# A two-layer graph network on one core: sums of a set of edges kept in parts of two chunks instead of five, one PSUM bank each

## The chip, the cores and the metric

The kernel runs on one core of a Trainium2 chip. The metric is the device time of one execution in microseconds (us). TensorE (PE in the profile) multiplies matrices into PSUM, VectorE (DVE) and ScalarE (ACT) work on SBUF and PSUM, GpSimd (POOL) issues the gathers, and SyncE (SP) issues the plain loads and stores.

## The reference

There are 6250 nodes with 256 features, 106,250 directed edges sorted by their target (one of them a loop of each node), and a type from 0 to 7 on each edge. A layer norm comes first, then three layers of a relational network, then a layer norm and one layer of attention:

```python
for l in range(n_layers):                          # 3 layers, R = 8 types, D = 256
    xr = jnp.einsum('nd,rde->rne', x, W_rel[l])
    msg = xr[edge_type, src]
    agg = jax.ops.segment_sum(msg, dst, num_segments=x.shape[0])
    x = jax.nn.relu(agg + x @ W_root[l] + bias[l])
...
h = x @ Wv + bv                                    # attention over the same edges
ex = exp(leaky_relu(h[src] @ wq + h[dst] @ wk) - max over the edges of a target)
out = segment_sum(h[src] * ex / sum(ex), dst)
```

## The kernel before

The kernel sums first and multiplies by the weights afterwards: for each target node and each type it adds up the rows of the sources, and then multiplies the eight sums by the eight matrices.

**Sets and chunks.** The 106,250 edges lie in 785 chunks of at most 128. A *set* is 14 chunks (45 sets), 13 chunks (11 sets) or 12 (the last), 57 in all; its targets span at most 128 nodes. The three layers walk the same list, `order`, of (set `t`, chunk `k`). All of this stage stands in a manual schedule: every engine runs its instructions in the order in which the Python code emits them.

**One chunk** (lines 1441 to 1518). GpSimd gathers the 128 source rows (`msg`, line 1097): each row is kept as three bf16 pieces, so that the sum of the pieces has full precision. VectorE makes a matrix of ones and zeros for two chunks at a time (`make_hots`, line 1408): column 8*n + r is one for the edges with target n and type r. TensorE multiplies the rows by it (`add`, line 1432): six bf16 matmuls, two halves of the features by three pieces, that add into `bank` in PSUM. The columns that a chunk can hit are known ahead: edges are sorted and the mean number of edges per node is known, so the position of a target wanders only so far (`nodes_before`). `near[k]` is the range of nodes that chunk k of a part can hit, counted from the part's first node; it becomes wider with k, as the wander adds up. With five chunks to a part, the matmuls are 104, 152, 168, 184 and 192 columns wide.

**Parts.** A part is `PART` = 5 chunks, that add into one `bank` (two PSUM banks of 2 KB, since there are 2 x 512 columns; the pool `gps` holds two such tiles). When a part is full, VectorE adds it to the set's sums `ag` in SBUF (`evacuate`, line 1313), one chunk later. The first part starts at node 0 of the set; the others start at a node that is known only on the chip: VectorE reads it into a register (`part_of`, line 1198: a register load and two register instructions in VectorE's queue), and `ag` is addressed by that register. The 14-chunk set has three parts and two such loads. An edge of the last chunk of the set before can belong to the first node of this one: six 8-column matmuls with `hot_p` open the first part.

**The rest of a set**, spread over the chunks that follow:

- `own_rows` (lines 1295 to 1305): chunk 0 and 1: TensorE turns the set's own rows (`pt`), ScalarE copies them (`x_t`, line 1298); chunks 2 to 4: eight VectorE instructions (line 1303) write the loops' share into `ag`. The additions of the parts come after them on VectorE.
- `finish(t)` (lines 1316 to 1379), while the chunks of set t+1 run: from chunk 2 to 10, two fp32 matmuls behind each chunk (lines 1335 and 1339; each shows as two matmuls in the profile), that read `ag`; at chunk 11 VectorE adds the bias (`v`, line 1344), then ScalarE and VectorE in turn make the three bf16 pieces (lines 1347 to 1353), which SyncE stores into the table of the next layer. In the last layer the second layer norm and the attention's columns are made here.
- In layer 0, besides: `count_loops`, and `norm_split` for one or two chunks of a set whose rows come from the input directly.

**Between layers.** The first set of a layer needs rows that the last set of the layer before makes. Its edges to the last 128 nodes are left out of its gathers and are counted apart in layer 0 (`count_late`) and added in set 1 of layers 1 and 2 (`add_late`).

Of the kernel before, what the change touches and what calls it, by code (L numbers as in the profile page):

```python
# [10 lines left out]
F32 = mybir.dt.float32  # L11
BF16 = mybir.dt.bfloat16
I32 = mybir.dt.int32
AF = mybir.ActivationFunctionType
ALU = mybir.AluOpType
AX = mybir.AxisListType
PSUM = bass.MemoryType.PSUM
DRAM = bass.MemoryType.DRAM

P = 128  # L20
# [8 lines left out]
LAST = 12  # L29
MORE = 20  # L30
PART = 5
SPREAD = 4.25
# [408 lines left out]
def kernel(  # L441
# [19 lines left out]
    nc = tc.nc  # L461
    N, D = x.shape
    E = src.shape[0]
    L, R = w_rel.shape[0], w_rel.shape[1]
    KH = D // P
# [225 lines left out]
    with tc.tile_pool(name="prep", bufs=1) as prep, \  # L691
# [80 lines left out]
        for n in ranges:  # L772
# [3 lines left out]
            for k, (lo, hi) in enumerate(ranges[n]):  # L776
                nc.gpsimd.memset(lows[n][:, k:k + 1], float(R * lo))
                nc.gpsimd.memset(lows_n[n][:, k:k + 1], float(ranges_w[n][k][0]))
                nc.gpsimd.memset(wides[n][:, k:k + 1], float(R * (hi - lo)))

        zero = nw.tile([P, 3 * D], BF16, bufs=1)
        nc.gpsimd.memset(zero, 0.0)
# [108 lines left out]
        def tables():  # L891
# [18 lines left out]
            firsts = prep.tile([1, NA, NW], F32)  # L910
            nc.vector.memset(firsts[:, 1:, NW - 1:], 0.0)
            nc.vector.tensor_copy(firsts[:, 0, :], base)
            for at, view, k in by_window(dst_t):
                for a in range(1, -(-k // PART)):
                    nc.vector.tensor_scalar_mul(firsts[:, a, at], view[0:1, :, a * PART], 1.0 / R)
            part_f = prep.tile([1, NA, NW], F32)
            nc.vector.tensor_tensor(part_f, firsts, base.unsqueeze(1).to_broadcast([1, NA, NW]),
                                    ALU.subtract)
            nc.vector.tensor_copy(part_i, part_f)
            b_ps = prep_ps.tile([P, NA, NW], F32)  # L920
            nc.tensor.matmul(b_ps.rearrange("p a w -> p (a w)"), ones[0:1],
# [8 lines left out]
            for (at, l_v, n), (_, d_v, _), (_, sg_v, _), (_, st_v, _), (_, o_v, _) in zip(  # L930
                    by_window(loc), by_window(dst_t), by_window(seg), by_window(seg_t),
                    by_window(over)):
                shape = [P, at.stop - at.start, n]
                nc.vector.scalar_tensor_tensor(
                    l_v, d_v, 1.0 / R, base_b[:, at].unsqueeze(2).to_broadcast(shape),
                    op0=ALU.mult, op1=ALU.subtract)
                for k in range(0, n, PART):
                    z = min(k + PART, n)
                    nc.vector.tensor_tensor(
                        sg_v[:, :, k:z], st_v[:, :, k:z],  # L940
                        seg_b[:, k // PART, at].unsqueeze(2).to_broadcast(shape[:2] + [z - k]),
                        ALU.subtract)
                nc.vector.tensor_tensor(sg_v, sg_v, lows[n].unsqueeze(1).to_broadcast(shape),
                                        ALU.subtract)
                nc.vector.tensor_tensor(o_v, sg_v, wides[n].unsqueeze(1).to_broadcast(shape),
                                        ALU.subtract)
                yield 1.5
# [19 lines left out]
            def at_most(a: bass.AP, most: float):  # L967
                v = next(vs)
                v = viol[:a.shape[0], v:v + 1]
                nc.vector.tensor_reduce(v, a, AX.X if len(a.shape) == 2 else AX.XY, ALU.max)  # L970
                nc.vector.tensor_scalar_add(v, v, -(most + 0.5))

            def at_least(a: bass.AP, least: float):
                v = next(vs)
                v = viol[:a.shape[0], v:v + 1]
                nc.vector.tensor_reduce(v, a, AX.X if len(a.shape) == 2 else AX.XY, ALU.min)
                nc.vector.tensor_scalar(v, v, -1.0, least - 0.5, op0=ALU.mult, op1=ALU.add)
# [36 lines left out]

            for a in range(1, NA):
                at_least(part_f[:, a, :NW - 1], float(far[a][0]))
                at_most(part_f[:, a, :NW - 1], float(far[a][1]))
            row = prep.tile([1, NW], F32)
# [66 lines left out]
    def ordered_path():  # L1085
# [23 lines left out]
        with ExitStack() as s:  # L1109
# [6 lines left out]
            one = s.enter_context(tc.tile_pool(name="ones", bufs=1))  # L1116
            gps = s.enter_context(tc.tile_pool(name="gps", bufs=2, space=PSUM))
            ops = s.enter_context(tc.tile_pool(name="ops", bufs=1, space=PSUM))
# [3 lines left out]
            FROM, UPTO = 2, CW - 3  # L1122
            STEPS = UPTO + 3
            RAW = 6

# [29 lines left out]
            nc.vector.tensor_scalar_add(seg_e, seg_e, -1e6)  # L1155
            late = one.tile([P, len(parts_e), P * R // 2], BF16)

# [26 lines left out]
            def add_late(a: int, xl, ag: bass.AP):  # L1184

                m = ranges[sizes[0]][parts_e[a][-1]][1]
                at = None if a == 0 else part_of(0, a)
                for h, name in zip(range(KH), ("pl", "pt")):
                    bank = ops.tile([P, P * R // 2], F32, name=name)
                    for s_ in range(3):  # L1190
                        nc.tensor.matmul(bank[:, :R * m], xl[:, s_, h * P:(h + 1) * P],
                                         late[:, a, :R * m], start=(s_ == 0), stop=(s_ == 2))
                    to = ag[:, h, :, :m] if at is None else ag[:, h, :, ds(at, m)]
                    nc.vector.tensor_tensor(
                        to, to, bank[:, :R * m].rearrange("p (n r) -> p r n", r=R), ALU.add)

# [119 lines left out]
            def finish(l: int, at, x_t: bass.AP, x0, ag: bass.AP, t: int):  # L1316
# [5 lines left out]
                if last and x0 is None:  # L1322
                    x0 = rp.tile([P, D], F32, name="x0")
                    nc.sync.dma_start(x0, x[ds(at, P), :])
                for _ in range(FROM if t or l == 0 else FROM + len(parts_e)):
                    yield
# [101 lines left out]
            def add(bank, msg, hot, lo: int, hi: int, begin: bool):  # L1428

                for h in range(KH):  # L1430
                    for s_ in range(3):
                        nc.tensor.matmul(  # L1432
                            bank[:, h, lo:hi], msg[:, s_, h * P:(h + 1) * P],
                            hot[:, :hi - lo], start=(begin and s_ == 0), stop=False,
                            skip_group_check=True)
# [3 lines left out]
            for l in range(L):  # L1439
                ahead = None  # L1440
                for i, (t, k) in enumerate(order):
# [18 lines left out]
                    if k % PART == 0:  # L1460
                        bank = gps.tile([P, KH, P * R // 2], F32, name="bank")

# [16 lines left out]

                    for c in to_copy:  # L1480
                        evacuate(*c)
                    to_copy = []
                    if k % PART == 0:
                        part_at = None if k == 0 else part_of(t, k // PART)
                    if k % PART == PART - 1 or k == n - 1:
                        to_copy.append((bank, ag, part_at, hi))
                    if l == 0 and final and k % 3 == 1 and k // 3 < len(parts_e):
                        count_late(k // 3)
                    if l and t == 0 and k == n - 1:
                        xl = rp.tile([P, 3, D], BF16, name="xl")  # L1490
                        nc.sync.dma_start(xl.rearrange("p s d -> p (s d)"), tab[l][LATE:N, :])
                        ag_e = ag
                    if l and t == 1 and 0 <= k - FROM < len(parts_e):
                        add_late(k - FROM, xl, ag_e)
                    if l == 0:
# [158 lines left out]
```

## Time and profile before

| | |
|---|---|
| time, three runs | median 5172.17 us (5154.45 to 5180.04) |
| profiled execution | 5168.06 us; its span 5166.3 us |
| granted TensorE clock, whole span | 0.859 |
| busy over the span | PE 3790.3 us, DVE 2766.0, ACT 1061.1, POOL 3044.0 |
| additions of parts (line 1313) | 513, mean 897 ns |
| chunk matmuls (line 1432) | 13668 recorded, 1362.7 us busy |

A *busy* time is the union of an engine's instructions, without register and queue instructions. In a group, the figures behind the bar are the busy time, the mean length of one in ns, and the idle time of the engine just before, with what ended it. In a timeline, the bracket is the idle time before an instruction and what ended it ("issue": nothing that the profile shows). The three layers run from about 235 to 3745 us, the attention from there to the end; before them lies the preparation of the edges.

### The profile page before, as it was taken

To read this page: it belongs to the slowest core of one execution; us is meant where nothing else is said; L and a number is where in the kernel's file an instruction comes from. 1 tells how busy PE (TensorE), PEld (TensorE's weight loads), DVE (VectorE), ACT (ScalarE), POOL (GpSimd) and SP (SyncE) were. 2 spreads that over 40 slices of the span, in tenths; PEclk is the share of its full clock that TensorE was granted. 3 is DMA by queue.
4 is the path that set the end of the run, shared out by engine and by line. 5 is a ranking of instruction groups with operands and counts; after the bars stand their busy time and mean duration, and the time that the engine had idled before them with its cause. 6 is when DMAs were issued, how large, how long until landed. Compare 5 with 4: busy or idle time off the path is not lost. (4 is left out here: it accounts for less than half of the span.)

```text
span 5166.3 us, 80833 instructions
## 1 busy us (share of the span) xinstructions
PE 3790.3 (73%) x28813; PEld 3179.2 (62%) x28813; DVE 2766.0 (54%) x7200; ACT 1061.1 (21%) x2620; POOL 3044.0 (59%) x3293
## 2 busy tenths in 40 slices
PE   0288888888687787778688888888845666666666
PEld 0277777777566666666566666666635655565556
DVE  5577766666344444444355555555534554555555
ACT  4421111111000000000000000000024444444444
POOL 6466666665566666666566666666555555555553
PEclk5599999999789999999888888889967887888888
DMA  4555555554455555555455555555533333333332
GB/s 120 191 149 150 149 151 148 171 167 140 123 150 151 149 153 149 149 150 150 130 152 160 159 157 158 158 159 159 137 86 89 93 90 91 96 94 97 92 98 62
DMA packets 302153, 694.32 MB, mean 134 GB/s; under 512 B 62677, under 2 KB 164501, under 8 KB 301739
## 3 DMA queue, kind: packets, MB, share of 16 engines
q0 software_dynamic: 188032, 562.89, 39.8%
q1 hardware_dynamic: 112650, 125.11, 7.8%
q8 instruction: 229, 3.75, 0.3%
q14 instruction: 186, 1.52, 0.1%
q10 hardware_dynamic: 1056, 1.05, 0.1%
HBM read 634.06 MB, written 54.78 MB: 133 GB/s over the span
## 5 line engine op out<-in xcount | busy, mean ns | idle before, releaser
L1097 POOL DMA_INDIRECT msg<-tab,src_t x2252 | 2166.1, 962 | 1312.9 <-PE bank L1432 520.1
L1432 PE MATMUL bank<-hots,msg 128*128 128x104 bf16 (+4 forms) x13668 | 1362.7, 241 | 250.7 <-issue 170.6
L1432 PEld LDWEIGHTS <-msg 128*128 128x128 bf16 x14556 | 1119.4, 102 | 641.5 <-issue 388.1
L1335 PE MATMUL po<-raws,ag 128*128 128x256 f32 x3648 | 1093.5, 427 | 172.2 <-DVE hots L1408 61.9
L1097 POOL DMA_INDIRECT head<-hx,src_t x785 | 745.2, 949 | 643.2 <-ACT qm L1564 189.3
L1313 DVE TENSOR_TENSOR ag<-ag,bank 128x768 f32<-128x768 f32 x513 | 460.1, 897 | 803.1 <-PE bank L1432 579.8
L1335 PEld LDWEIGHTS po<-raws,ag 128*128 128x128 f32 x3648 | 693.2, 211 | 273.1 <-issue 75.4
L1303 DVE SCALAR_TENSOR_TENSOR ag<-loops,x_t 128x256 f32<-128x256 bf16 x1368 | 494.9, 420 | 390.6 <-issue 289.2
L1408 DVE TENSOR_TENSOR hots<-up,seg 128x304 bf16<-128x304 f32 (+4 forms) x1182 | 585.5, 506 | 32.6 <-PE bank L1432 17.6
L1335 PE MATMUL po<-wr,ag 128*128 128x256 f32 x1824 | 544.4, 422 | 38.7 <-issue 19.6
L1594 PE MATMUL pf<-ex,head 128*128 128x128 f32 x3364 | 486.5, 312 | 101.1 <-issue 55.5
L1594 PEld LDWEIGHTS pf<-ex,head 128*128 128x128 f32 x3364 | 472.0, 227 | 114.6 <-issue 60.5
L1335 PEld LDWEIGHTS po<-wr,ag 128*128 128x128 f32 x1824 | 332.9, 203 | 82.4 <-issue 31.7
L1564 ACT ACTIVATE qm<-other,head 128x128 f32<-128x128 f32 x841 | 283.1, 396 | 108.1 <-issue 42.0
L1570 DVE TENSOR_REDUCE tops<-pq 128x1 f32<-128x512 f32 x228 | 154.9, 679 | 217.4 <-ACT c L1569 161.4
L1566 PE MATMUL pq<-ident,qm 128*128 128x128 f32 x898 | 186.4, 316 | 114.7 <-issue 44.5
L563 ACT ACTIVATE std<-mv,eps 128x1 f32<-128x1 f32 x134 | 39.6, 296 | 1089.0 <-DVE mv L561 724.9
L1347 ACT ACTIVATE hml<-v 128x256 bf16<-128x256 f32 x114 | 47.6, 418 | 1023.4 <-issue 756.1
L1555 DVE TENSOR_SCALAR other<-up,loc 128x128 f32<-128x128 f32 x785 | 237.8, 341 | 13.2 <-ACT qm L1564 6.9
L1585 PE MATMUL pe<-ident,c 128*128 128x128 f32 x898 | 162.9, 325 | 94.6 <-issue 51.9
L1602 PE MATMUL po<-wv_s,fs 128*128 128x256 f32 x228 | 87.8, 523 | 190.4 <-ACT fs L1599 127.6
L1566 PEld LDWEIGHTS pq<-ident,qm 128*128 128x128 f32 x898 | 127.1, 160 | 161.0 <-ACT qm L1564 77.2
(259 smaller groups left out, 3133.3 us busy)
## 6 DMA issues: line engine op xcount, KB each, us to landing
msg<-tab,src_t POOLq DMA_INDIRECT x2252
xt<-tab SPq DMA_DIRECT2D x171, 192.0 KB
tab<-hml SPq DMA_DIRECT2D x114, 192.0 KB
head<-hx,src_t POOLq DMA_INDIRECT x785
tab<-hml SPq DMA_DIRECT2D x12, 768.0 KB
hx<-row SPq DMA_DIRECT2D x57, 128.5 KB
mine<-hx SPq DMA_DIRECT2D x57, 128.5 KB
xa<-x SPq DMA_DIRECT2D x57, 128.0 KB
```

Of the source, the lines that this page charges most:

```text
L1097: nc.gpsimd.indirect_dma_start(out=to, out_offset=None, in_=table[:upto, :], in_offset=bass.IndirectOffsetOnAxis(ap=index, axis=0))
L1303: nc.vector.scalar_tensor_tensor(ag[:, :, r, :m], loops[:, t, :m].unsqueeze(1).to_broadcast([P, KH, m]), float(r + 1), x_t[:, :, :m], op0= ...
L1313: nc.vector.tensor_tensor(to, to, bank[:, :, :R * m].rearrange("p h (n r) -> p h r n", r=R), ALU.add)
L1335: nc.tensor.matmul(po[:m], ag[:, h, r, :m], wr[:, h, r, :], start=(r == 0 and h == 0), stop=False, skip_group_check=True)
L1408: nc.vector.tensor_tensor(pair[:, :n, :width], up[:, :width].unsqueeze(1).to_broadcast([P, n, width]), of[:, i:i + n].unsqueeze(2).to_broa ...
L1432: nc.tensor.matmul(bank[:, h, lo:hi], msg[:, s_, h * P:(h + 1) * P], hot[:, :hi - lo], start=(begin and s_ == 0), stop=False, skip_group_c ...
L1555: nc.vector.tensor_scalar(other[:, :m], up[:, :m], refs[j][1], None, op0=ALU.not_equal)
L1564: nc.scalar.activation(qm[:, :m], other[:, :m], AF.Identity, scale=MASKED, bias=refs[j][0][:, D:HX])
L1566: nc.tensor.transpose(pq[:m, i, :], qm[:, :m], ident)
L1570: nc.vector.tensor_reduce(tops[:m, g:g + 1], flat, AX.X, ALU.max)
L1585: nc.tensor.transpose(pe[:, i, :m], c_t[:m, j * P:(j + 1) * P], ident[:m, :m])
L1594: nc.tensor.matmul(pf[:, h, :m], refs[j][0][:, h * P:(h + 1) * P], ex[:, i, :m], start=(j == 0 and h == 0), stop=(j == len(refs) - 1 and h ...
```

## The change

A part has two chunks. Its columns fit one PSUM bank, and four such tiles are in hand instead of two of two banks. A 14-chunk set has seven parts, so seven additions and six register loads. Parts of the current set wait until chunk 5 (`READY`), when the own rows are in place; from then on at most one part is added in a chunk. Late edges are counted two parts, and added three parts, in one chunk step, and both halves of a late part share one PSUM tile. The checks of the parts' first nodes are reduced over all parts at once.

```diff
-PART = 5
+PART = 2
...
-            gps = s.enter_context(tc.tile_pool(name="gps", bufs=2, space=PSUM))
+            gps = s.enter_context(tc.tile_pool(name="gps", bufs=4, space=PSUM))
...
+            READY = 5
...
-                for h, name in zip(range(KH), ("pl", "pt")):
-                    bank = ops.tile([P, P * R // 2], F32, name=name)
+                bank = ops.tile([P, P * R // 2], F32, name=("pl", "pt")[a % 2])
+                bank = bank.rearrange("p (h c) -> p h c", h=KH)
+                for h in range(KH):
...
+                evacuate(bank, ag, at, m)
...
-                for _ in range(FROM if t or l == 0 else FROM + len(parts_e)):
+                for _ in range(FROM if t or l == 0 else FROM + LATE_STEPS):
...
-                            hot[:, :hi - lo], start=(begin and s_ == 0), stop=False,
+                            hot[:, :hi - lo], start=(begin and h == 0 and s_ == 0), stop=False,
...
-                        bank = gps.tile([P, KH, P * R // 2], F32, name="bank")
+                        bank = gps.tile([P, KH, P * R // 4], F32, name="bank")
...
-                    for c in to_copy:
-                        evacuate(*c)
-                    to_copy = []
+                    for c in to_copy[:len(to_copy) if k < READY else 1]:
+                        if k >= READY or c[1] is not ag:
+                            evacuate(*c)
+                            to_copy.remove(c)
                     if k % PART == 0:
                         part_at = None if k == 0 else part_of(t, k // PART)
                     if k % PART == PART - 1 or k == n - 1:
                         to_copy.append((bank, ag, part_at, hi))
-                    if l == 0 and final and k % 3 == 1 and k // 3 < len(parts_e):
-                        count_late(k // 3)
+                    if l == 0 and final and k % 3 == 1:
+                        for a in range(k // 3 * 2, min(k // 3 * 2 + 2, len(parts_e))):
+                            count_late(a)
...
-                    if l and t == 1 and 0 <= k - FROM < len(parts_e):
-                        add_late(k - FROM, xl, ag_e)
+                    if l and t == 1 and 0 <= k - FROM < LATE_STEPS:
+                        for a in range((k - FROM) * 3, min((k - FROM) * 3 + 3, len(parts_e))):
+                            add_late(a, xl, ag_e)
```

`near` is computed from `PART`; its two ranges are now 0 to 13 and 3 to 22 nodes, so the chunk matmuls are 104 and 152 columns wide in turn, and a full part has 2 x 176 columns (352) where it had 2 x 384 (768).

## The prediction

> **What bounds the kernel now.** I read the page's rows of 40 slices first, then the table by stage, then the waits of one layer, then one set of that layer in order of time.
>
> ```profile
> 235.00:1285.00 1050.00, 913.55 (x7935) 766.08 (x7935) 713.61 (x1760) 167.88 (x495) 653.57 (x677) 0.94 0.54 153
> 1401.00:2502.00 1101.00, 881.87 (x6930) 715.29 (x6928) 520.97 (x1167) 76.18 (x212) 697.21 (x728) 0.93 0.53 150
> 2617.00:3730.00 1113.00, 911.18 (x6931) 749.54 (x6929) 604.51 (x1646) 80.33 (x212) 700.85 (x728) 0.88 0.58 158
> ```
>
> These are layers 0, 1 and 2 without their seams: length, busy PE, PEld, DVE, ACT, POOL, then granted clock, DMA share, GB/s. TensorE is busiest (80 to 87%), but nothing is full: gathers fill 62 to 63% of GpSimd, VectorE is at 47 to 68%. So a loop of waits sets the pace. The longest waits of TensorE in layer 1:
>
> ```profile
> PE bank L1432 <- issue: 125.4, 242, 1.3
> PE po L1335 <- DVE hots L1408: 46.1, 28, 2.0
> PE bank L1432 <- DMA msg<-tab,src_t: 3.1, 4, 1.2
> ```
>
> The columns are us in total, times, longest. One set of that layer, by start and length in us:
>
> ```profile
> 1998.10 2.07 PE L1335 MATMUL po<-raws,ag 128*128 128x256 f32 x4 [1.59 <-DVE hots L1408]
> 2002.03 0.37 ACT L1298 COPY x_t<-pt 128x256 f32<-128x256 f32 x1 [5.64 <-PE bank L1432]
> 2005.81 0.96 DVE L1313 TENSOR_TENSOR ag<-ag,bank 128x768 f32<-128x768 f32 x1
> 2007.95 0.64 PE L1432 MATMUL bank<-hots,msg 128*128 128x184 bf16 x6
> 2009.32 0.66 PE L1432 MATMUL bank<-hots,msg 128*128 128x192 bf16 x6
> 2010.71 0.44 PE L1432 MATMUL bank<-hots,msg 128*128 128x104 bf16 x6
> 2010.98 1.09 PE L1339 MATMUL po<-raws,x_t 128*128 128x256 f32 x4
> 2012.63 0.95 DVE L1313 TENSOR_TENSOR ag<-ag,bank 128x768 f32 x1 [4.12 <-PE bank L1432]
> 2013.64 0.17 PE L1432 MATMUL bank<-hot_p,msg 128*128 128x8 bf16 x1 [0.26 <-issue]
> 2015.59 0.42 DVE L1344 TENSOR_TENSOR v<-po,raws 128x256 f32<-128x256 f32 x1 [2.00 <-remote]
> 2017.44 0.43 DVE L1353 TENSOR_TENSOR hml<-v,hml 128x256 bf16<-128x256 f32 x1 [0.47 <-ACT hml L1351]
> 2018.25 0.81 DVE L1313 TENSOR_TENSOR ag<-ag,bank 128x640 f32 x1
> 2019.12 0.79 PE L1335 MATMUL po<-raws,ag 128*128 128x256 f32 x1 [1.14 <-DVE hots L1408]
> ```
>
> Gathers are no limit (3.1 us in a layer). The set shows the loop. `finish` starts at 1998.10 and its last matmuls end at 2012.07 (14.0 us); `v` on VectorE starts at 2015.59 (3.5 us later); from there VectorE makes `v` and `hml` and then adds the last part, which ends at 2019.06 (3.5 us); the next `finish` starts 0.06 us later. 14.0 + 3.5 + 3.5 = 21.0 us, the period. Going through all sets of the timeline so, the loop is 19.1 / 20.7 / 20.9 us in layers 0 / 1 / 2: finish 14.0 / 14.0 / 13.7, lag up to `v` 0.75 / 3.1 / 2.0, chain 4.4 / 3.5 / 5.2; in nearly every set `finish` starts 0.05 us after the last addition. Only what lies in these three terms counts. The lag is odd: VectorE and ScalarE see TensorE's results late (`x_t` 5.6 us idle, part 1's addition 2.7 us after its last matmul). In layers 1 and 2, `hot_p` stalled for its bank in 47 of 108 sets; there the lag is 3.5 us, in the others 1.9.
>
> **The change part by part.**
>
> *Narrower matmuls.* Six matmuls of 192 columns take 0.66 us, of 104 columns 0.44: 0.22 / (6 x 88) = 0.42 ns a column. A 14-chunk set falls from 2208 columns to 1792 for each of its six matmuls a chunk; all sets of the three layers save 418,752 columns x 0.42 = 175 us of TensorE's time. Only chunks 3 to 10 lie inside `finish`: 1280 columns become 1024, 6 x 256 x 0.42 = 0.64 us; taken as 0.65 a set. The rest (0.4 us a set) lies in chunks after which TensorE waits for VectorE anyway.
>
> *The bank that `hot_p` waits for.* With four tiles and seven parts it needs part 3, added at chunk 8, so the 0.3 to 0.9 us wait goes. Late next is the last part, as now. What the lag does then is not shown: from nothing to 1.6 us a stalled set (3.5 - 1.9). I take 0.5 a set in layer 1 (39 of 54 stall), 0.1 in layer 2 (8 of 54), none in layer 0 (1 of 55).
>
> *More additions, and register loads.*
>
> ```profile
> L1313 DVE TENSOR_TENSOR ag<-ag,bank 128x768 f32 x171 | 163.2, 954 | 606.0 <-PE bank L1432 486.4 <-PE po L1339 59.8 <-remote 40.7
> L1313 DVE TENSOR_TENSOR ag<-ag,bank 128x496 f32 x33 | 22.0, 665 | 8.1 <-PE bank L1432 5.0 <-PE pt L1295 2.0 <-remote 1.1
> L1408 DVE TENSOR_TENSOR hots<-up,seg 128x304 bf16<-128x304 f32 x338 | 158.4, 469 | 32.5 <-PE bank L1432 17.6 <-remote 10.6 <-PE pl L1278 3.5
> L1198 DVEq TENSOR_LOAD <-part_i x346: 298/306/324, 205.6 to 3747.2; - x173
> L1198 DVEq FUSED_REGOPS  x346: 190/190/206, 206.0 to 3747.6; - x173
> ```
>
> 289 ns for 272 elements: 1.06 ns each and 136 ns for the instruction. A part of 352 is 0.51 us; seven are 3.6 us against 2.7 for three. `hots` falls by 320 elements, 0.3 us. Six loads for two: a load starts only when the addition ahead of it starts, and takes 0.31 + 0.19 us with gaps, so the instruction behind starts some 0.85 us after that addition. A 0.96 us addition hides it; a 0.51 us one leaves 0.4 us open, at least 0, at most the whole 0.85. I take 0.4: VectorE gets 0.6 + 6 x 0.4 = 3 us more work a set. Most of it falls between chunks 6 and 10, where VectorE idled 4.1 us. If that cover is gone (layer 0's first 20 sets: 289 us busy in 385), it costs up to its length; I take 0.5 us for those 20 sets, 10 us.
>
> In the chain, part 5's addition and a load now stand between `v` and the second step of `hml`; ScalarE's `hml` (and with it SyncE's store) waits behind it. `v` 0.34, `hots` 0.39, addition 0.1 + 0.51, load 0.35, step two 0.43, wait for ScalarE 0.47, step three 0.34, `hots` 0.39, last part 0.5: 3.8 to 3.9 against 3.47 us. I take +0.4 in each layer (0 to +0.85, by the load).
>
> *A new wait at chunk 8.* Its tile is part 0's, added at chunk 5 behind the own rows, that wait for the late `x_t`. Now that addition ends before chunk 8's matmuls start by a median of 1.7 / 0.6 / 2.2 us in the three layers. The chunk comes 0.34 us earlier (136 columns saved in chunks 3 to 7), the addition 0.4 later (0.45 shorter, two exposed loads). So layer 1 loses its slack in half its sets: +0.2 a set; 0 in the others.
>
> *Late edges, preparation.* Seven late parts in set 1: 7 x (0.51 + 0.4) against six additions (0.55 or 0.41) and two loads: +2.5 us in each of two layers. `count_late` takes 14 of the 22 `msg` tiles where it took 8: the gathers on POOL run less far ahead in one set, +2 us (0 to 5). 12 small GpSimd fills and a few fewer VectorE instructions in the preparation: 0 (-2 to +2). No other transfer moves on SP or POOL, and the attention is untouched.
>
> *The clock.* The rows grant 0.94, 0.93, 0.88. The Trainium skill, "TensorE: Matmul & The Clock Gate", section "A second HAM failure mode: psum-queue depth-cycling", speaks against the change: a kernel that cycles through PSUM banks idles TensorE briefly and often, and its clock oscillates. Seven tiles a set in place of three would, by that, bring layer 1 to something like layer 2's 0.88: 14 us x (1/0.88 - 1/0.93) = 0.85 us a set, +145 us over three layers. The trace weakens it: layer 0, with 1 stall for a bank in 55 sets, has 0.94, layer 1, with 39 in 54, 0.93. I take 0 and keep the rest for the range.
>
> Sum a set: layer 0 -0.65 + 0.4 = -0.25; layer 1 -0.65 - 0.5 + 0.4 + 0.2 = -0.55; layer 2 -0.65 - 0.1 + 0.4 = -0.35. Times 57: -14, -31, -20; with +10 and +7, -48 us. Against the profiled execution's 5168 us (span 5166 and 2 around it; 4 below the median of the runs): 5120 us.
>
> **The rivals.**
>
> *VectorE's additions come late (slower).* Place: chunk 8's tile. Each load costs 0.85 us and not 0.4, and the own rows start no earlier, so part 0 is ready 1.3 us later. It decides once part 0 ends over 0.6 us later in layer 1, 1.7 in layer 0. Layer 1 then loses 1.3 - 0.3 = 1.0 a set, layer 0's first 20 sets 1.5 each, and the chain 0.4 more in all sets: 57 + 30 + 68 = 155 us. With all of it, less the 21 that I have counted, 5120 + 134 = 5254; with two thirds, 5210. For it: `x_t`'s 5.6 us, and 75% busy VectorE at the start. Against: 4.1 us idle later in the same set.
>
> *The lag goes (much faster).* If the late signals come from the bank stalls, layers 1 and 2 get layer 0's 0.75 us: 57 x (3.1 - 0.75 + 2.0 - 0.75) = 205 us, of which I counted 34. Half of the rest more gives 5120 - 85 = 5035. For it: 3.5 against 1.9 us. Against: 1.9 without a stall, so something else delays most of it.
>
> *It doesn't show.* TensorE's saved columns end up in front of the same last addition: only if loads and chunk 8 eat the 0.65: 5165.
>
> **How the numbers follow.** Main case 45% (5060 to 5170), late additions 27% (5210), lag gone 18% (5035), nothing 10% (5165). Half a per cent, 26 us, is about what a measurement of this kernel can tell. Below 5142: 0.31 of the main case, all of the lag's, none of the others: about 0.50. Above 5194: 0.27 and a tail of 0.03: 0.30. Same: 0.20. The range 5000 to 5235 takes in half the lag's full gain and the late case with a load's upper bound; a clock at 0.88 is left out. Where it is faster, 5035 to 5140.
>
> **What would show it.** Right: chunk matmuls of 104 and 152 columns alone; `finish` about 13.4 us; no idle time before `hot_p` by a bank; additions near 0.51 us; the last addition still 0.05 us ahead of `finish`; `v` to last addition near 3.9 us. Wrong: TensorE waiting for `ag` L1313's successor at chunk 8 by more than 0.3 us a set; a lag in layer 1 near 0.75 or above 3.5 us; a granted clock under 0.90 in layers 0 and 1; VectorE's loads exposed by 0.8 us.

## The result, and the profile after

| comparison | kernel before, us | changed kernel, us | ratio, 95% interval |
|---|---|---|---|
| the first (20 runs each) | 5155.09 | 5183.26 | 1.0047 [1.0034, 1.0061] |
| again, second chip | 5169.47 | 5187.21 | 1.003 [1.0016, 1.0044] |
| again, another chip | 4156.59 | 4136.84 | 0.9953 [0.994, 0.9966] |

The change costs 28 us (0.5%, clear of the interval) where I forecast a gain of 48 against the profiled execution. The sign is wrong, though 5183 lies in the range of 5000 to 5235. The experiments fell on chips of two kinds, which have to be told apart in all that follows: *late* chips (the first comparison and three later groups of runs; the kernel before takes 5086 to 5169 us) and *prompt* chips (two groups; 4155 and 4157 us). On a prompt chip the same change gains 0.5%.

The three layers after the change, in the table by stage (length, busy PE, PEld, DVE, ACT, POOL, granted clock, DMA share, GB/s):

```profile
235.00:1285.00 1050.00, 888.51 (x7890) 731.06 (x7891) 732.90 (x1973) 160.83 (x495) 649.13 (x672) 0.91 0.53 152
1401.00:2502.00 1101.00, 890.82 (x6893) 710.09 (x6893) 541.02 (x1367) 68.26 (x208) 697.89 (x727) 0.85 0.53 150
2617.00:3730.00 1113.00, 881.00 (x6914) 711.22 (x6913) 625.29 (x1847) 73.31 (x212) 699.08 (x728) 0.84 0.57 157
```

TensorE has 175 us less to do at full clock, and yet in layer 1 it is busy for longer than before (890.82 against 881.87 us): the granted clock fell from 0.94, 0.93 and 0.88 to 0.91, 0.85 and 0.84. (In the trace it is either full or half, half for 1617 us in all.) VectorE has 20 us more in each layer. One column hardly moved: GpSimd, 697.89 us for 727 instructions in layer 1, nearly all of them gathers, before 697.21 for 728. The longest waits of TensorE in layer 1 (us in total, times, longest):

```profile
PE bank L1448 <- issue: 101.0, 193, 1.2
PE po L1351 <- DVE ag L1329: 32.4, 21, 2.1
PE pt L1311 <- issue: 28.1, 48, 1.2
PE po L1351 <- issue: 19.7, 25, 1.8
```

The wait of `hot_p` for its bank is gone (0.30 us a set in layer 1 before, 0.00 now), but 193 stops with no named releaser remain at the chunk matmuls. One set of layer 1, by start and length:

```profile
1991.21 2.07 PE L1351 MATMUL po<-raws,ag 128*128 128x256 f32 x4 [1.70 <-DVE hots L1424]
...
1999.37 0.29 PE L1448 MATMUL bank<-hots,msg 128*128 128x152 bf16 x2
1999.90 0.42 PE L1448 MATMUL bank<-hots,msg 128*128 128x152 bf16 x4 [0.23 <-issue]
...
2003.86 1.09 PE L1355 MATMUL po<-raws,x_t 128*128 128x256 f32 x4
2006.08 0.52 DVE L1329 TENSOR_TENSOR ag<-ag,bank 128x352 f32 x1 [2.42 <-PE bank L1448]
...
2006.78 0.39 PE L1448 MATMUL bank<-hots,msg 128*128 128x104 bf16 x5
2007.59 0.47 PE L1448 MATMUL bank<-hots,msg 128*128 128x104 bf16 x5 [0.41 <-issue]
2007.62 0.42 DVE L1360 TENSOR_TENSOR v<-po,raws 128x256 f32<-128x256 f32 x1 [1.02 <-PE bank L1448]
2008.35 0.30 PE L1448 MATMUL bank<-hots,msg 128*128 128x152 bf16 x2 [0.29 <-issue]
2009.99 0.43 DVE L1369 TENSOR_TENSOR hml<-v,hml 128x256 bf16<-128x256 f32 x1 [0.47 <-ACT hml L1367]
2012.13 0.52 DVE L1329 TENSOR_TENSOR ag<-ag,bank 128x352 f32 x1 [1.33 <-PE pt L1311]
2012.71 0.79 PE L1351 MATMUL po<-raws,ag 128*128 128x256 f32 x1 [0.25 <-issue]
```

The loop still closes: finish 1991.21 to 2004.95, `v` 2.7 us later, the next finish 0.06 us after the last addition. But TensorE breaks off in the middle of a group of six matmuls (2006.78 to 2007.59, after the fifth) where nothing is left to wait for in the program. The means over the sets of a layer, without the first and the last ones, in us:

| | period | finish | lag | chain |
|---|---|---|---|---|
| layer 0, before and after | 19.06, 19.19 | 13.98, 13.86 | 0.76, 1.07 | 4.32, 4.27 |
| layer 1 | 20.66, 20.83 | 14.04, 13.92 | 3.13, 2.55 | 3.50, 4.35 |
| layer 2 | 20.89, 21.04 | 13.69, 13.47 | 2.02, 2.32 | 5.20, 5.27 |

Each set is 0.13 to 0.17 us longer: 57 x (0.13 + 0.17 + 0.15) = 26 us, nearly the whole loss. The groups of VectorE (busy us, mean ns | idle before) and its loads (min/median/max ns):

```profile
L1329 DVE TENSOR_TENSOR ag<-ag,bank 128x352 f32 x990 | 511.9, 517 | 724.0 <-PE bank L1448 435.3 <-remote 134.4 <-PE po L1355 45.6
L1424 DVE TENSOR_TENSOR hots<-up,seg 128x304 bf16<-128x304 f32 x1147 | 531.3, 463 | 4.0 <-issue 3.9
L1214 DVEq TENSOR_LOAD <-part_i x1035: 297/304/686, 184.6 to 3780.2; - x173
```

### The profile page after: what moved, and what is told of

Its sections match the earlier page's. It is cut to its first block, busy times and chain, and to the rows that moved or that the text cites. A ratio compares the mean times of both kernels' runs of the same rounds, so it can differ in the third digit from the quotient of the medians.

```text
span 5184.2 us, 85281 instructions
## 1 busy us (share of the span) xinstructions
PE 3769.6 (73%) x28861; PEld 3114.9 (60%) x28861; DVE 2841.9 (55%) x7881; ACT 1040.5 (20%) x2624; POOL 3045.1 (59%) x3305
## 3 DMA queue, kind: packets, MB, share of 16 engines
q10 hardware_dynamic: 1056, 1.05, 0.1%
## 5 line engine op out<-in xcount | busy, mean ns | idle before, releaser
L1448 PE MATMUL bank<-hots,msg 128*128 128x104 bf16 (+1 forms) x13668 | 1220.6, 231 | 290.3 <-issue 204.6
L1448 PEld LDWEIGHTS <-msg 128*128 128x128 bf16 x14556 | 1012.2, 104 | 654.9 <-issue 393.6
L1351 PE MATMUL po<-raws,ag 128*128 128x256 f32 x3648 | 1182.3, 454 | 164.7 <-DVE ag L1329 75.9
L1329 DVE TENSOR_TENSOR ag<-ag,bank 128x352 f32 (+2 forms) x1194 | 613.0, 513 | 751.1 <-PE bank L1448 444.0
L1351 PEld LDWEIGHTS po<-raws,ag 128*128 128x128 f32 x3648 | 739.3, 225 | 271.4 <-DVE ag L1329 88.8
L1351 PE MATMUL po<-wr,ag 128*128 128x256 f32 x1824 | 568.5, 436 | 41.8 <-issue 21.0
L1424 DVE TENSOR_TENSOR hots<-up,seg 128x304 bf16<-128x304 f32 (+1 forms) x1182 | 540.4, 457 | 4.4 <-issue 4.2
L1351 PEld LDWEIGHTS po<-wr,ag 128*128 128x128 f32 x1824 | 343.9, 209 | 89.3 <-issue 34.1
L1311 PE MATMUL pt<-ident_b,xt 128*128 128x128 bf16 x1026 | 128.2, 232 | 139.3 <-issue 122.5
```

The source lines that it names most:

```text
L1329: nc.vector.tensor_tensor(to, to, bank[:, :, :R * m].rearrange("p h (n r) -> p h r n", r=R), ALU.add)
L1351: nc.tensor.matmul(po[:m], ag[:, h, r, :m], wr[:, h, r, :], start=(r == 0 and h == 0), stop=False, skip_group_check=True)
L1424: nc.vector.tensor_tensor(pair[:, :n, :width], up[:, :width].unsqueeze(1).to_broadcast([P, n, width]), of[:, i:i + n].unsqueeze(2).to_broa ...
L1448: nc.tensor.matmul(bank[:, h, lo:hi], msg[:, s_, h * P:(h + 1) * P], hot[:, :hi - lo], start=(begin and h == 0 and s_ == 0), stop=False, s ...
```

## The experiments

Theory A is the prediction's: finish, lag and VectorE's chain set the period. Theory B: the clock takes back what narrower matmuls save. Theory C came from the two traces: whatever the three terms do, a set takes the same time for each chunk that GpSimd gathers (1.51 to 1.56 us). Theory D: TensorE's own work sets the pace where its results are seen late. The first four runs had no run of the changed kernel beside them; the later one on a prompt chip (0.9953) is their measure.

### The chain shortened

```diff
                 nc.vector.tensor_add(v[:m], po[:m], bb[:m])
+                for _ in range(3):
+                    yield
```

> The changed kernel with three steps inserted in finish between v and what follows it, so that hml (and the last layer's moments) stands behind the last part's addition on VectorE and not ahead of it. Output unchanged. Theory A (the loop finish, lag, chain, with VectorE's chain lengthened by the change): the chain loses hml's two steps and the wait for ScalarE between them, 0.43 + 0.47 + 0.34 = 1.2 us in layers 0 and 1 and some 2 us in layer 2, 57 x (1.2 + 1.2 + 2.0) = 250 us less than the changed kernel: about 4930 us. Theory B (TensorE's half-rate windows take back what narrower matmuls save): TensorE waits less for the last addition, so the clock in layers 1 and 2 rises above 0.88 and the time falls by at least what A says. Theory C (a set takes 1.51 us for each chunk that GpSimd gathers, whatever TensorE and VectorE do: 14 gathers 21.1, 13 gathers 19.7, layer 0 with 12 gathers 18.6): no change, 5183 within 15, and the lag grows by what the chain loses.

On a prompt chip: 4135.35 us, 0.9949 [0.9932, 0.9965] of the kernel before, which is what the changed kernel has by itself (0.9953). Theory A's 250 us did not come. The same edit on a late chip:

> The changed kernel with hml behind the last addition, as in the first experiment. The kernel before did not gain by it (0.9993) where results are seen late. Theory A: 1.2 to 2 us less in each set's chain, 0.96. Theories C and D: 1.000 to 1.004 there, since the lag takes back what the chain loses; 0.995 on the other chip.

The ratio is 1.0039 [1.0023, 1.0056]: nothing gained. And in the kernel before, on a late chip:

> The kernel before with the three inserted steps of the first experiment (hml and the last layer's moments behind the last addition). Output unchanged. If the first experiment's gain (0.5%) came from the loop of finish and chain in layer 2, which both kernels have, it is 0.4 to 0.8% here too. If it only took back what the change had added to the chain, it is under 0.2%. Theory C: nothing, within 0.2%.

The ratio is 0.9993 [0.9979, 1.0006]. Beside the kernel before on that chip, the chain in layer 2 fell from 5.17 to 3.27 us, and in its place the lag grew from 2.07 to 2.96 and finish from 13.73 to 14.62: the period went from 20.94 to 20.87. Three terms that add up to the period, and one taken away without effect: the sum is an identity, not a cause.

### TensorE kept at work

```diff
+                if l:
+                    fill = ops.tile([P, P * R // 2], F32, name="pl")[:, :2 * R * near[-1][1]]
+                    for i in range(8):
+                        nc.tensor.matmul(fill, ident_b, late[:, 0:2, :].rearrange("p a c -> p (a c)"),
+                                         start=True, stop=True)
                 po = ops.tile([P, D], F32, name="po")
```

> The changed kernel with eight matmuls of 352 columns in bf16 (8 x 0.147 = 1.2 us) ahead of each finish in layers 1 and 2, where TensorE waits for the last addition. They go to a bank that is not used there and is not read; output unchanged. Theory B: TensorE no longer idles there, the granted clock goes from 0.85 and 0.84 to 0.95 or more in layers 1 and 2, finish from 13.8 to about 12.5 us, and the time falls by some 57 x 2 x 1.0 = 110 us to 5070. Theory A: the filler lies in a wait, nothing changes but what of it sticks out, 5183 to 5230. Theory C: the clock rises and the time stays, 5183 within 15; the lag grows.

On a prompt chip 4142.68 us, 0.9971 [0.9951, 0.999]. The granted clock inside layers 1 and 2 rose from 0.94 and 0.90 (the changed kernel on the other prompt chip) to 0.97 and 0.98, and finish fell from 12.40 and 12.61 us to 11.41 and 11.70. The time did not follow (4137 without the filler), and theory B's 110 us did not come. In layer 1 finish is not what counts: the period stayed at 17.4 us. Layer 2 decides nothing, because the filler stands between the last addition and finish: the way from `v` to the next finish grew from 5.03 to 5.84 us and ate what finish gained.

### Fewer gathers

In layers 1 and 2 the kernel leaves out the gathers of chunks 5 and 10; their matmuls read the rows of the chunk ahead once more, so the sums are wrong.

```diff
+                    elif l and t and k in (5, 10):
+                        msg = ahead
```

> The changed kernel without the gathers of chunks 5 and 10 in layers 1 and 2 (but set 0): their matmuls read the tile of the chunk ahead again, so this part of the sums is wrong; all else is as it was. Theory C: a set of 14 takes 12 x 1.51 = 18.1 us where it took 21.1, 56 x 2 x 3.0 = 340 us less: about 4845. Theories A and B: gathers are waited for only 3 us in a layer, so nothing changes: 5183 within 20.

Prompt chip: 4017.35 us, 0.9664 [0.9648, 0.9681], 120 us below the changed kernel. Theory C had said 340, at a late chip's pace. Layer 1 fell from 17.4 to 15.0 us a set; layer 2 stayed (17.7 and 17.8). With fewer gathers layer 2 is held by finish, lag and chain (12.84 + 0.04 + 4.95 us), so on a prompt chip C is right for layer 1 and wrong for layer 2.

> The changed kernel without the gathers of chunks 5 and 10 in layers 1 and 2, as in the third experiment (this part of the sums is wrong). On the chip where TensorE's results are seen late (the kernel before 5160 us): theory C, 2 x 1.51 us less in 112 sets, 340 us, ratio 0.93; theories A and D: within 0.5% of the changed kernel. On the chip where they aren't (the kernel before 4155 us): 0.966 as before.

Late chip: 4822.25 us, 0.9475 [0.9449, 0.95]. Against the kernel with hml later on the same chip (5108 us) that is 286 us in 112 sets, 2.55 us for two gathers, where C had 3.0. No other edit moved the time like this. In layer 1 the sets with 14 chunks take 18.1 us, 12 gathers at the old pace of 1.51, as C has it; layer 2 is then held by finish, lag and chain (12.8 + 0.5 + 5.0 us). TensorE changed as well: finish fell from 14.0 and 14.2 us to 12.7 and 12.8 in layers 1 and 2, the lag from 2.2 and 2.7 to 1.8 and 0.5, and the stops without a name became fewer. Its weight loads from 1401 to 2100 us, with hml later, then with fewer gathers:

```profile
PEld L1450 <- issue: 113.9, 208, 2.0
```

```profile
PEld L1448 <- issue: 63.1, 115, 1.3
```

The edit takes away the traffic of two gathers, TensorE's wait for their rows and its release of their tiles at once; no run separates them.

### Half of finish left out

```diff
-                todo = [(r, h) for r in range(R) for h in range(KH)] + [(R, h) for h in range(KH)]
+                todo = [(r, 0) for r in range(R)] + [(R, h) for h in range(KH)]
```

> The changed kernel with finish cut from 36 to 20 fp32 matmuls (the second half of the features is left out of the products with the relations' weights, so the outputs are wrong). 16 x 0.215 us = 3.4 us less TensorE work inside finish in each set at full clock. Theory A (loop of finish, lag, chain) and theory D (TensorE's own work sets the pace where its results are seen late): up to 3.4 us less in each of 171 sets, 580 us, at least 2 us (340) before something else binds. Theory C (gathers set the pace, on either chip): 0 in layers 0 and 1, and in layer 2 at most the 0.35 us (20 us) by which it lies above 14 gathers. Theory B: the clock falls and takes back a part.

The kernel leaves out the second half of the features in the products with the relations' weights. Late chip: 5056.57 us, 0.993 [0.9909, 0.9951]; against 5108 us, 51 us, or 0.30 us a set of the 3.4 taken out. Layer 1 and TensorE's longest waits in it (1401 to 2100 us):

```profile
1401.00:2502.00 1101.00, 771.90 (x6146) 593.73 (x6145) 551.04 (x1401) 70.41 (x214) 692.92 (x723) 0.79 0.52 150
```

```profile
PEld L1448 <- issue: 208.7, 354, 2.0
```

In layer 1 finish takes 11.62 us, the lag 4.32 and the period is still 20.4. TensorE has less to do, but it breaks off more often at the chunks' weight loads (209 us in 354 stops, where the kernel with hml later has 114 in 208), and the granted clock is 0.79. A falls with this, and so does D as far as it means the amount of TensorE's work. That TensorE's stops and late results pace the sets on a late chip is not excluded.

### The old number of columns on the new structure

```diff
+                for _ in range(0 if hi - lo == R else 2 if lo == 0 else 1):
+                    nc.tensor.matmul(
+                        bank[:, 0, lo:hi], msg[:, 0, :P], hot[:, :hi - lo], start=False,
+                        stop=False, skip_group_check=True)
```

> The changed kernel with one or two more matmuls for each chunk, which repeat the first third of the first half (152 or 2 x 104 columns), so that its columns a set are 1792 + 420 = 2200 in units of six matmuls, as before the change; that third of the sums counts twice or three times. Theory A (every column inside finish counts): 4 x 2 x 104 + 4 x 152 = 1440 columns in finish, 1440 x 0.42 ns = 0.6 us a set wherever the loop sets the pace, 34 us a layer; 34 us more if that is layer 2 alone, 100 if all. Theory B: the clock rises with the columns and the time stays, within 10 us of the changed kernel. Theory C: 0 in layers 0 and 1.

Late chip: 5222.32 us, 1.0111 [1.0074, 1.0147], 35 us above the changed kernel on that chip. Layers 1 and 2, first of the changed kernel, then with the columns back:

```profile
1401.00:2502.00 1101.00, 889.84 (x6883) 712.50 (x6881) 539.13 (x1367) 68.35 (x208) 698.47 (x727) 0.84 0.52 150
2617.00:3730.00 1113.00, 881.54 (x6916) 711.83 (x6916) 625.30 (x1848) 73.69 (x213) 698.33 (x728) 0.84 0.57 157
```

```profile
1401.00:2502.00 1101.00, 903.40 (x7903) 730.56 (x7903) 535.47 (x1352) 68.09 (x208) 691.15 (x718) 0.92 0.52 148
2617.00:3730.00 1113.00, 906.05 (x7822) 742.95 (x7822) 614.94 (x1818) 71.63 (x208) 685.87 (x716) 0.88 0.56 155
```

2520 more columns a set are 1.05 us at full clock, but busy PE grows by 14 and 25 us only in these windows, while the clock rises (0.84 to 0.92 and 0.88). What is left is 35 / 171 = 0.20 us a set, where theory C had nothing. So the narrower matmuls seem to have gained some 35 us on a late chip, give or take 20. And the structure by itself, with equal columns, cost 5222 - 5169 = 53 us. (Four runs; the interval leaves 38 to 76.) The edit gives the columns back as further matmuls (7903 in layer 1, not 6883), and the kernel before had wider ones. What the mere number of instructions costs is in both figures, and no run takes it out.

### Loads and additions apart

```diff
-                return nc.vector.value_load(part_i[0:1, a, t:t + 1], min_val=far[a][0],
-                                            max_val=far[a][1])
+                return far[a][0]
```

> The changed kernel with a constant in place of the position that VectorE loads from memory for each part (no register loads; the parts' sums go to slightly wrong places). Theory A with the loads as the dear part: 0.35 us less in the chain of each set and more ahead of chunk 8, 57 x 3 x 0.35 = 60 us less: 5123. Theory B: no change of the clock, 5183 within 20. Theory C: 5183 within 15, the lag grows by what the chain loses.

> The changed kernel with constants in place of the positions that VectorE loads (sums go to slightly wrong places). On the chip where results are seen late the changed kernel is at 1.003 to 1.005 of the kernel before. If the register loads are what the structure costs (the changed kernel with its old number of columns was at 1.011): 6 loads of 0.3 to 0.5 us a set open on VectorE, 0.2 us a set, 35 us: ratio 0.996. If the additions and their waits are the cost: 1.003 to 1.005. On the other chip: 1.000.

> The changed kernel with constants in place of the positions that VectorE loads (sums go to slightly wrong places), beside the changed kernel on one chip. If the six loads a set are what remains of the cost: 0.996 of the changed kernel, level with the kernel before. If the four more additions are: the same as the changed kernel within 0.1%.

Constants take the place of the loaded positions, so some sums go to wrong places. On a late chip 0.9996 [0.9977, 1.0015], where the kernel that differs by the loads and the three steps had 1.0039: 18 us for the six loads a set, give or take 13. On prompt chips 1.0004 [0.9996, 1.0013] and 1.0003 [0.9995, 1.0011], which is 20 us slower than the changed kernel (0.9953). Work taken from VectorE made the time longer there, where I had expected the changed kernel's time or 0.4% less; I have no cause for this. The other way round, loads or additions alone put into the kernel before:

```diff
+                    if k in (2, 4, 8, 12):
+                        part_of(t, 1)
```

> The kernel before with four more loads of a position a set (at chunks 2, 4, 8 and 12; their values are not used), so that it has the six of the changed kernel. Output unchanged. If the loads are the cost: 1.003 to 1.004. If the additions are: 1.000 within 0.1%.

> The kernel before with four more loads of a position a set, as in the thirteenth run, for a chip where TensorE's results are seen late (the kernel before at 5090 to 5170 us). There the changed kernel was at 1.003 and 1.0047, and without its loads at 0.9996. If the loads are the cost, 1.003 to 1.005; if not, 0.999 to 1.001. On the other kind of chip (4155 us) 1.0016 as before.

```diff
-                to = ag[:, :, :, :m] if at is None else ag[:, :, :, ds(at, m)]
-                nc.vector.tensor_tensor(
-                    to, to, bank[:, :, :R * m].rearrange("p h (n r) -> p h r n", r=R), ALU.add)
+                for h in range(KH):
+                    to = ag[:, h, :, :m] if at is None else ag[:, h, :, ds(at, m)]
+                    nc.vector.tensor_tensor(
+                        to, to, bank[:, h, :R * m].rearrange("p (n r) -> p r n", r=R), ALU.add)
```

> The kernel before with each part's addition made as two, one for each half of the features: six additions a set and not three, with the same banks, columns and loads. Output unchanged. VectorE gets 3 x 136 ns and some register work, 0.5 to 0.8 us a set, and 0.2 us of that in the chain. If additions are the cost of the change: 1.002 to 1.004. If the loads are: 1.000 within 0.1%. Theory A: 171 x 0.2 = 34 us, 1.007.

> The kernel before with each part's addition made as two, as in the fourteenth run, for a chip where results are seen late. If VectorE's additions and their waits are the cost there, 1.002 to 1.005; if the loads are, 0.999 to 1.001. On the other kind of chip 0.9985 as before.

Loads: 1.0016 [1.0001, 1.0032] on a prompt chip, 1.001 [0.9995, 1.0025] on a late one. Additions: 0.9985 [0.9978, 0.9992] and 0.9996 [0.9983, 1.0008]. Additions as such cost nothing that shows. Four loads cost at most 13 us on a late chip, and the 1.003 that I had expected if loads are the cost was reached on neither. The change adds four, not six, and two thirds of 18 is 12, so the two tests do not contradict each other. Of the structure's 53 us, at most some 13 are put down to loads; the rest is open.

### The changed kernel again, and the pace of the gathers

> The changed kernel itself, beside the kernel before on one chip, as the run that the others are held against: in the first experiments the kernel before took 4155 us and not 5155, and VectorE saw TensorE's results 0.04 us after their end and not 0.75 to 3.1. Theory C (a set takes what its gathers take, 1.26 us each there): layers 0 and 1 as before the change, so a ratio of 0.997 to 1.003. Theory A: layer 2, where the last addition still precedes finish by 0.06 us, changes by 0.35 us a set at most, 20 us (0.5%) to either side. If TensorE's results are seen late again, the ratio is 1.003 to 1.006 as in the first comparison.

> The kernel before, for its trace beside that of the changed kernel on the same chip. Theory C: GpSimd gathers without a pause in layers 0 and 1, 1.26 us a gather and 17.6 us a set of 14, as in the changed kernel. Theory A: a period of 17.5 to 18.5 us in layer 2, set by finish, lag and chain. Theory B: a clock above that of the changed kernel by 0.03 or more in layers 1 and 2.

> The changed kernel itself, so that the three runs beside it have their measure on the same chip. Where TensorE's results are seen late (the kernel before at 5090 to 5170 us) 1.003 to 1.005; on the chip where they aren't (4155) theory C says 0.998 to 1.002.

The changed kernel is at 1.003 of the kernel before on the late chip and at 0.9953 on the prompt one, where theory C had 0.998 to 1.002; what gains 20 us there is open. The kernel before (5180.55 us, one run) was traced on a late chip, so its prompt trace is missing; it repeated the first trace (periods 19.17, 20.72 and 20.94 us). GpSimd in layer 1 of the changed kernel, late chip first (start, length, idle before in the bracket):

```profile
1806.04 1.10 POOL L1111 DMA_INDIRECT msg<-tab,src_t  x1 [0.31 <-issue]
1807.44 1.08 POOL L1111 DMA_INDIRECT msg<-tab,src_t  x1 [0.30 <-issue]
1808.83 0.95 POOL L1111 DMA_INDIRECT msg<-tab,src_t  x1 [0.30 <-issue]
1810.08 0.95 POOL L1111 DMA_INDIRECT msg<-tab,src_t  x1 [0.30 <-issue]
1812.36 0.94 POOL L1111 DMA_INDIRECT msg<-tab,src_t  x1 [1.33 <-PE bank L1448]
...
1818.39 0.94 POOL L1111 DMA_INDIRECT msg<-tab,src_t  x1 [1.34 <-PE bank L1448]
```

```profile
1806.41 0.94 POOL L1111 DMA_INDIRECT msg<-tab,src_t  x1 [0.30 <-issue]
1807.66 0.94 POOL L1111 DMA_INDIRECT msg<-tab,src_t  x1 [0.30 <-issue]
1808.91 0.94 POOL L1111 DMA_INDIRECT msg<-tab,src_t  x1 [0.30 <-PE bank L1448]
1810.15 0.95 POOL L1111 DMA_INDIRECT msg<-tab,src_t  x1 [0.30 <-PE bank L1448]
1811.40 0.95 POOL L1111 DMA_INDIRECT msg<-tab,src_t  x1 [0.30 <-PE bank L1448]
```

On the prompt chip the gathers run on without a break, 1.25 us from start to start here and 1.27 in the mean (553 in the 700 us from 1300 on). 14 make 17.8 us and 13 make 16.5; the sets of layer 1 take about as long. On the late chip each gather is as long, but after four of them comes a pause of 1.3 us instead of 0.3: 6.03 us for four, 1.51 for one. 14 make 21.1 us. The sets with 14 gathers take about 21.1 us before and 21.2 after in layer 1, those with 13 about 19.7 in both. In layer 0, of the sets with 14 chunks, those with 12 gathers take 18.5 and 18.6 (medians), those with 13 gathers 19.8 and 19.9. TensorE's work on the chunks is the same in these last two; the 12 are the first sets, in which VectorE and ScalarE prepare one more chunk. On the prompt chip these two kinds of sets differ by 0.1 us only (16.0 and 16.1, means). The longest wait of the weight loads in layer 1 (1401 to 2100 us), late, then prompt:

```profile
PEld L1448 <- issue: 110.0, 194, 1.3
```

```profile
PEld L1448 <- DMA msg<-tab,src_t: 142.3, 178, 2.4
```

On the prompt chip TensorE waits for gathered rows, as it should when gathers set the pace. There a chunk's matmuls in layer 1 start 3.2 us (median) after GpSimd's instruction for its rows has ended, 3 gathers behind.

On the late one its waits have no name, and GpSimd is not what it waits for. A chunk's matmuls start 27 us after the end of its gather (median, both traces of the changed kernel), 18 gathers behind, while the rows land 2.0 us after that end (median; 5.6 at most, in the records that the trace has). They lie ready for some 20 us. GpSimd has 22 tiles for rows, and its pauses are waits for TensorE to give one back: of the 102 pauses over 0.6 us from 1401 to 2100 us, 95% end within 0.15 us after a signal of TensorE. GpSimd's waits in that stretch, late, then prompt:

```profile
POOL msg L1111 <- PE bank L1448: 98.4, 102, 2.2
```

```profile
POOL msg L1111 <- PE bank L1448: 64.3, 211, 0.3
```

So on a late chip it is shown that a set's time goes with the number of its gathers, but not why: TensorE has its rows, and GpSimd waits for TensorE. The two often stand still together: from 1401 to 2502 us GpSimd's pauses fill 21% of the time, and 46% of the time in which TensorE stops among the chunk matmuls without a name. The loading of instructions does not cover these stops: its packets (queues q8 and q14) run in 5.3% and 1.6% of that stretch, and in 6.1% and 1.5% of the stops' time.

## Why the prediction was wrong, point by point

- *"Only what lies in these three terms counts"*: this is the step that failed. The loop closes in every kernel traced on a late chip, but as long as every chunk is gathered its terms do not set its period there. The chain was cut by 1.9 us in layer 2, and the period fell by 0.07; finish was cut by 2.3 us in layer 1, and the period fell by 0.4. The lag takes up the difference. I called it odd, and then took 0.5 us a set from it as a gain. What the period does follow is the number of gathers in a set: 2.55 us for two on a late chip.
- *"Gathers are no limit (3.1 us in a layer)"*: as a reading of TensorE's waits this was right, and the rows did lie ready. But I concluded that gathers cost nothing, and passed over the longest row of the same list, 125.4 us in 242 stops with "issue". On a prompt chip gathers are the limit in layer 1. On a late chip they cost time in another way, which stays open.
- *Narrower matmuls, -0.65*: finish fell by 0.12, 0.12 and 0.22 us. The columns were counted rightly; while the clock fell, finish kept most of its length. In time the columns are worth some 0.20 us a set, with the doubt named above.
- *The clock, 0*: wrong. The Trainium skill's page "TensorE: Matmul & The Clock Gate", section "A second HAM failure mode: psum-queue depth-cycling", ties an oscillating clock to short idle spells of TensorE between groups of matmuls; from it I had estimated 0.88 in layer 1, and measured were 0.85 and, on the second chip, 0.84. But going through seven banks does not do it alone: with the same banks and the columns back the clock was at 0.92. With half of finish out it was 0.79. Nor is it the amount of work alone: with hml later the kernel before had 0.90 and 0.92 in layers 1 and 2, where it has 0.93 and 0.88. The price was not the 145 us that I worked out, since the period does not follow finish.
- *The bank of `hot_p`, -0.5 in layer 1*: as mechanism right, 0.30 to 0.00, and the lag fell by 0.58. It bought no time.
- *Chain +0.4*: -0.05, +0.85 and +0.07. In layer 1 it was my upper end. On the period it had no part on a late chip, as the two runs with hml later show.
- *VectorE's loads and additions*: the additions cost nothing that shows; the four more loads cost at most some 13 us on a late chip, where I had them hidden or in the chain. That the new structure could cost 53 us was in no term. *Late edges and preparation, +7*: not tried.
- *Rivals*: in microseconds "it doesn't show" (5165, 10%) lies nearest, but the prediction counts from 5168: a loss of 28 us lies nearer to the late additions (5210), and that is luck. The late additions at chunk 8 did not come: in the first trace TensorE is idle ahead of chunk 8 for under 0.01 us a set. The lag did not go.
- Of the signs that I named for being wrong, the clock under 0.90 came in layer 1 only; its 0.91 in layer 0 was close.

The balance on a late chip: columns -35 us, structure +53, together +18, which is the 5187 - 5169 of that group. It has to come out so, since the 53 was found as the difference; of the 53, some 40 have no cause yet. The first comparison had 28; the two intervals overlap.

## What to carry to other kernels

When the terms of a loop add up to its period, that proves nothing: vary one suspect and see whether the period follows (here sets with 12, 13 and 14 gathers were in the trace before any experiment). A lag that nothing explains takes up what is saved elsewhere, so gains counted against it vanish. Stops put down to "issue" are unexplained time, not harmless time: the longest row of a wait list must be accounted for before a shorter one is priced. And a count that the period follows is not yet a cause: see whether the results are waited for, by how far ahead they were made.

## What was not expected of the hardware

Single instructions run equally fast on the two kinds of chips, where compared: a gather takes 962 ns on a late chip and 970 on a prompt one, a part's addition 513 ns on both. What differs is the time between them, and with it the whole kernel by 24%:

```profile
L1111 POOL DMA_INDIRECT msg<-tab,src_t x2252 | 2167.3, 962 | 1349.4 <-PE bank L1448 520.4
```

```profile
L1111 POOL DMA_INDIRECT msg<-tab,src_t x2252 | 2185.0, 970 | 716.7 <-issue 316.1
```

Late first: 1349 against 717 us of idle time before the gathers. There VectorE sees TensorE's results 0.8 to 3.1 us after their end (0.04 on a prompt chip, in layers 1 and 2), GpSimd pauses after about four gathers, and TensorE stops within groups of six matmuls. Of the engines' signals it is TensorE's that come late: in layer 1 they are recorded at least 0.74 us (median) after the recorded end of the matmul that sends them, on the prompt chip 0.014; those of VectorE and ScalarE come about 0.01 us after the end on both. What makes a chip late is open; no run changed it.

The granted clock in layer 1 fell with the change (0.93 to 0.85), and more matmuls on the same structure raised it (0.84 to 0.92). And on a prompt chip the changed kernel without its loads took 4158 us, with them 4137.
